# Stores given out some microseconds behind their producers in a graph-attention kernel of two layers

## The chip, the cores and the metric

The kernel runs on one core of one Trainium2 chip, in float32 throughout. Its time is the device time of one execution in microseconds (us). The core has five engines that run their own instruction streams in order: TensorE (PE, matrix products; its weight loads are listed apart as PEld), VectorE (DVE), ScalarE (ACT), GpSimd (POOL) and SyncE (SP), which computes nothing and here hands out nearly all DMA transfers. An instruction of one engine waits for another engine, or for a transfer, by a semaphore. PSUM is the small memory that PE writes its results to, SBUF the memory that all engines work in, DRAM the large memory outside.

## The reference

There are 128 batches of 128 nodes with 512 features. Layer 0 normalises, mixes the nodes by the adjacency matrix and multiplies by one weight. Layer 1 is masked attention with 8 heads and a projection, followed by a second normalisation.

```python
# layer 0
h = relu(layernorm(x))
x = x + (einsum('nm,bmd->bnd', adj, h) @ weight + bias)          # this x is called x1 below
# layer 1
h = relu(layernorm(x))                                           # called h1 below
q, k, v = split_heads(h @ w_qkv)                                 # 8 heads of 64
p = softmax(where(adj == 0, -inf, q @ k.T / 8))                  # the probabilities
o = (p @ v) @ w_proj + b_proj
x = x + o + layernorm(o) * gamma + beta
```

## The kernel before

The program is one long list of steps. `put(t, f, ...)` files a step under a nominal time `t` in us; at the end all steps are called in the order of these times, and each call appends its instructions to the engines' streams. So `t` sets only the order in every stream, SyncE's included, and not when anything runs. One batch has a slot of 17.8 nominal us; even and odd batches form pairs. Large products are done in a form with seven block products instead of eight, with sums of blocks made on POOL (`ysum`, `hsum`, `osum`).

A transfer appended to SyncE's stream in the step that also appends its producer stands there from that place on, and SyncE hands out nothing behind it until the producer is done. The parts that the change touches:

```python
    def exchange(t, b, dst=None):                 # 128x128 blocks are turned by a trip through DRAM
        w = b.shape[2]
        d = dram.tile([P, Q, w], F32, name=f"d{w}")
        nc.sync.dma_start(out=d, in_=b)           # L220: the store
        put(t, exchange_back, b if dst is None else dst, d)

    def exchange_back(dst, d):                    # L225: four reads, each for 32 partitions
        for q in range(Q):
            nc.sync.dma_start(out=dst[q * R:(q + 1) * R, :, :], in_=d[:, q, :].rearrange("(n r) w -> r n w", n=Q))

    def norm1_out(i, t, arg):                     # h1 of batch i
        h1 = H1[i] = work.tile([P, Q, C, R], F32, name="h1", bufs=4)
        nc.scalar.activation(h1..., X[i]..., AF.Relu, **arg)                        # L327
        exchange(t + 4.5, h1.rearrange("p q c r -> p q (c r)"))
        put(t + (1.5 if i >= AHEAD else 0), keep_x1, i)                             # AHEAD = 8

    def keep_x1(i):
        if i >= AHEAD:
            nc.gpsimd.tensor_tensor(X[i], X[i], beta_b, op=ALU.add)                 # L335
        X1D[i] = dram.tile([P, D], F32, name="x1d", bufs=20)
        nc.sync.dma_start(out=X1D[i], in_=X.pop(i))                                 # L337

    def softmax_mask(i, ps):                      # ps: scores in PSUM
        s = late(0) if spare(i) else work.tile([P, Q, H * R], F32, name="s", bufs=2)
        ...
        nc.vector.tensor_tensor(s..., ps[e]..., m4, op=ALU.add)                     # L401, then maximum L406

    def spare(i):
        return i > LATE + 2 and i % 2             # LATE = 120: batches 123, 125, 127

    def late(n):                                  # two places in a tile that is no longer in use
        if not LATER:
            t = work.tile([P, C, G, P], F32, name="h1T")...
            LATER.extend(t[:, n]... for n in range(2))
        return LATER[n]

    def softmax_divide(i, t, e, sm):
        nc.vector.reciprocal(sm, sm)                                                # L433
        nc.gpsimd.tensor_tensor(e, e, sm..., op=ALU.mult)                           # L435
        S[i] = late(1) if spare(i) else work.tile([P, Q, H * R], F32, name="sx", bufs=1)
        exchange(max(t + 5, read_at(i)), e.rearrange("p q h r -> p q (h r)"), S[i])

    def flip_probs(i):
        PT[i] = work.tile([P, 2 * C, P], F32, name="pT", bufs=2)
        nc.vector.transpose(PT[i]..., S.pop(i)...)                                  # L441

    def finish_out(i, t, arg):
        n = O.pop(i)
        nc.scalar.activation(n, n, AF.Identity, **arg)                              # L490
        put(t + 1.5, lambda: nc.gpsimd.tensor_tensor(n, n, gamma_b, op=ALU.mult))   # L491
        put(t + 3, finish_last, i, n, X1B.pop(i))

    def finish_last(i, n, x1):
        if i < AHEAD:
            nc.gpsimd.tensor_tensor(n, n, beta_b, op=ALU.add)                       # L496
        nc.gpsimd.tensor_tensor(n, n, x1, op=ALU.add)                               # L497
        nc.sync.dma_start(out=out[i], in_=n)                                        # L498
```

Other lines that the profile names: L285-286 the mixing (`pmix`), L300 the block products of layer 0 and of the projection (`pd`, `pz`), L263 and L306 DVE's emptying of their PSUM banks, L372 the block products for q, k and v (`pc`, `pz`), L376 ACT's emptying of them, L392 the scores (`ps`), L425 the exponentials, L450 the attention product (`po`), L468 whole products at the head and the tail, L159 the fetching of a weight block (`wq`), L479 the reloading of x1 (`x1b<-x1d`), L485 its sum with `o`.

Of the kernel before, what the change touches and what calls it, by code (L numbers as in the profile page):

```python
# [9 lines left out]
F32 = mybir.dt.float32  # L10
# [4 lines left out]
P = 128  # L15
# [5 lines left out]
def kernel(  # L21
# [30 lines left out]
    nc = tc.nc  # L52
    B, N, D = x.shape
    H = 8
    HD = D // H
    C = D // P
    G = 4
    Q, R = 4, 32
# [5 lines left out]
    work = ctx.enter_context(tc.tile_pool(name="work", bufs=2))  # L64
# [6 lines left out]
    LATER = []  # L71
    X, H0, YT, X1D, H1, H1T, WQ, QKT, V, S, PT, OT, O, X1B, LEFT0, LEFT1, LEFT2 = ({} for _ in range(17))
# [139 lines left out]

        return shifts, [dict(bias=shift[:, n:n + 1], scale=rs[:, n:n + 1]) for n in range(w)]

    def exchange(t, b, dst=None):


        w = b.shape[2]
        d = dram.tile([P, Q, w], F32, name=f"d{w}")
        nc.sync.dma_start(out=d, in_=b)  # L220
        put(t, exchange_back, b if dst is None else dst, d)

    def exchange_back(dst, d):
        for q in range(Q):
# [93 lines left out]
    def norm1(j, t):  # L318
        pair = 2 * j, 2 * j + 1
        shifts, args = stats_of([X[i] for i in pair])  # L320
        put(t + 3, shifts)
        for n, (i, arg) in enumerate(zip(pair, args)):
            put(t + 3 + n, norm1_out, i, t + 3 + n, arg)

    def norm1_out(i, t, arg):
        h1 = H1[i] = work.tile([P, Q, C, R], F32, name="h1", bufs=4)
        nc.scalar.activation(h1.rearrange("p q c r -> p c q r"), X[i].rearrange("p (c q r) -> p c q r", c=C, q=Q),  # L327
                             AF.Relu, **arg)
        exchange(t + 4.5, h1.rearrange("p q c r -> p q (c r)"))
        put(t + (1.5 if i >= AHEAD else 0), keep_x1, i)  # L330

    def keep_x1(i):

        if i >= AHEAD:
            nc.gpsimd.tensor_tensor(X[i], X[i], beta_b, op=ALU.add)  # L335
        X1D[i] = dram.tile([P, D], F32, name="x1d", bufs=20)
        nc.sync.dma_start(out=X1D[i], in_=X.pop(i))  # L337


    def flip(i):  # L340
# [43 lines left out]
    def scores(i, t):  # L384

        g, j = divmod(i, G)
        qk = QKT[g][j // 2]
        ps = [psum.tile([P, C, P], F32, tag="at", name=f"ps{e}", bufs=4) for e in range(2)]
        for c in range(C):
            for e in range(2):  # L390
                r = slice(e * HD, (e + 1) * HD)
                nc.tensor.matmul(ps[e][:, c, :], lhsT=qk[r, c, j % 2, :], rhs=qk[r, C + c, j % 2, :],  # L392
                                 start=True, stop=True)
        put(t + 1, softmax_mask, i, ps)

    def softmax_mask(i, ps):
        s = late(0) if spare(i) else work.tile([P, Q, H * R], F32, name="s", bufs=2)
        s = s.rearrange("p q (h r) -> p h q r", h=H)
        m4 = maskb.rearrange("p (q r) -> p q r", q=Q).unsqueeze(1).to_broadcast([P, C, Q, R])
        for e in range(2):  # L400
            nc.vector.tensor_tensor(s[:, e * C:(e + 1) * C], ps[e].rearrange("p c (q r) -> p c q r", q=Q), m4, op=ALU.add)  # L401
        put(softmax_at(i), softmax_max, i, softmax_at(i), s)
# [6 lines left out]
    def spare(i):  # L409
        return i > LATE + 2 and i % 2  # L410

    def late(n):

        if not LATER:
            t = work.tile([P, C, G, P], F32, name="h1T").rearrange("p (n c) j m -> p n (c j m)", n=2)
            LATER.extend(t[:, n].rearrange("p (q w) -> p q w", q=Q) for n in range(2))
        return LATER[n]

    def softmax_exp(i, t, s, shift):
        nc.scalar.mul(shift, shift, -scale)  # L420
        sm = stat.tile([P, H], F32, name="sm")

        def exps(heads):
            for h in heads:
                nc.scalar.activation(s[:, h], s[:, h], AF.Exp, bias=shift[:, h:h + 1], scale=scale,  # L425
                                     accum_out=sm[:, h:h + 1])

        exps(range(H // 2))
        put(t + 2, exps, range(H // 2, H))
        put(t + 4.2, softmax_divide, i, t + 4.2, s, sm)  # L430

    def softmax_divide(i, t, e, sm):
        nc.vector.reciprocal(sm, sm)  # L433
        e = e.rearrange("p h q r -> p q h r")
        nc.gpsimd.tensor_tensor(e, e, sm.unsqueeze(1).unsqueeze(3).to_broadcast([P, Q, H, R]), op=ALU.mult)  # L435
        S[i] = late(1) if spare(i) else work.tile([P, Q, H * R], F32, name="sx", bufs=1)
        exchange(max(t + 5, read_at(i)), e.rearrange("p q h r -> p q (h r)"), S[i])

    def flip_probs(i):
        PT[i] = work.tile([P, 2 * C, P], F32, name="pT", bufs=2)  # L440
# [40 lines left out]
    def finish(batches, t):  # L481
        shifts, args = stats_of([O[i] for i in batches])
        put(t + 3, shifts)
        for n, (i, arg) in enumerate(zip(batches, args)):
            put(t + 1 + 3 * n, lambda i=i: nc.gpsimd.tensor_tensor(X1B[i], X1B[i], O[i], op=ALU.add))  # L485
            put(t + 3 + 3 * n, finish_out, i, t + 3 + 3 * n, arg)

    def finish_out(i, t, arg):
        n = O.pop(i)
        nc.scalar.activation(n, n, AF.Identity, **arg)  # L490
        put(t + 1.5, lambda: nc.gpsimd.tensor_tensor(n, n, gamma_b, op=ALU.mult))  # L491
        put(t + 3, finish_last, i, n, X1B.pop(i))

    def finish_last(i, n, x1):
        if i < AHEAD:
            nc.gpsimd.tensor_tensor(n, n, beta_b, op=ALU.add)  # L496
        nc.gpsimd.tensor_tensor(n, n, x1, op=ALU.add)  # L497
        nc.sync.dma_start(out=out[i], in_=n)  # L498

# [6 lines left out]
    BEGIN, LAST, AHEAD = -3, B - G, 8  # L508
# [3 lines left out]
    def put(t, f, *a):  # L512
        count[0] += 1
        heapq.heappush(later, (t, count[0], f, a))

    def when(i, us):
        return i * SLOT + us if i >= 0 else i * SHORT + us * SHORT / SLOT

    def mix_at(i):
        return START + i * STEP if i < AHEAD else when(i - 10, (11.6, 9.2)[i % 2])  # L520
# [24 lines left out]
    LATE = LAST - G  # L545
    AT = {key: [] for key in "asQpD"}
    t, last = when(LATE, 0), ""
# [11 lines left out]
    def softmax_at(i):  # L559
        if i < LATE:  # L560
            return when(i, 0.5) if i % 2 else scores_at(i) + 3
        return TAIL + (5, 13, 26, 35, 58, 63.5, 70.5, 76)[i - LATE]

    def read_at(i):
        if i < LATE:
            return when(i + 1, 9) if i % 2 else 0
        return TAIL + (16, 24, 37, 46, 69, 74.5, 81.5, 87)[i - LATE]
# [6 lines left out]
    def attend_at(i):  # L574
        return when(i - i % 2 + 4, i % 2) if i < LATE - 4 else AT["a"][i - LATE + 4]
# [11 lines left out]
    for j in range(B // 2):  # L587
        a, b = 2 * j, 2 * j + 1
        i = a - 8
        if a < AHEAD:  # L590
            t = mix_at(a) - (8.5 if a else 5)
            put(t, norm0, j, t)
            for n in (a, b):
                t = mix_at(n) + 5.2
# [3 lines left out]
        else:  # L598
            t = when(i - 3, 5.2)
            put(t, norm0, j, t)  # L600
            t = when(i - 1, 12)
            put(t, pair_left, j, t, 2.5, YT, LEFT0, "ysum")
            run(lambda j=j: layer0(j), [when(i, p) for p in PAIR[0]])
            t = when(i, PAIR[0][6]) + 1.5
# [5 lines left out]
        i = a + 5  # L610
        t = attend_at(b) + 2
        if b < LAST:
            put(t, pair_left, j, t, 3.4 if i < LATE else 1.5, OT, LEFT2, "osum")
            n = 7 * (a - LATE + 4) // 2
# [3 lines left out]
        else:  # L618
            ends = []
            for n in (a, b):  # L620
                t = AT["D"][n - LAST]
# [8 lines left out]
    for g in range(B // G):  # L630
        i = g * G - 3
        t, gap = (START + 36.2, 1.4) if g == 0 else (when(i - 1, 13), 4) if i < LATE else (TAIL + 9.8, 2.2)
        put(t, group_left, g, t, gap)
        times = sorted(when(i + n, p) for n in range(G) for p in GROUP[(i + n) % 2] + ((13.1,) if n == 0 else ()))
        if i + G > LATE:
            n = sum(t < TAIL for t in times)
# [24 lines left out]
    while later:  # L661
        t, _, f, a = heapq.heappop(later)
# [30 lines left out]
```

## Time and profile before

| what | value |
|---|---|
| time, median of 3 runs | 2372.13 us (2368.23 to 2372.77) |
| span of the profiled execution | 2374.6 us |
| mean granted clock of TensorE | 0.996 |
| DMA moved | 518.86 MB, 218 GB/s |
| share of the time of 16 DMA engines taken by SyncE's queue | 68.7% |
| PE idle, by windows of 50 us: 0 to 150 us | 9.1 us |
| PE idle, 2250 us to the end | 23.3 us |

The profile's page lists busy time by engine, the waits of each engine with what ended them, the chain of work that ended last, and groups of instructions by source line. A line of the waits reads "engine tile line <- releaser tile line: us in total, times, longest us". SPq is the queue of SyncE. An entry such as "[4.89 <-DMA d<-h1T]" gives the idle time of the engine just before that instruction and what ended it. "a<-b" names the tile written and the tile read.

### The profile page before, as it was taken

To read this page: it belongs to the slowest core of one execution; us is meant where nothing else is said; L and a number is where in the kernel's file an instruction comes from. 1 tells how busy PE (TensorE), PEld (TensorE's weight loads), DVE (VectorE), ACT (ScalarE), POOL (GpSimd) and SP (SyncE) were. 2 spreads that over 40 slices of the span, in tenths; PEclk is the share of its full clock that TensorE was granted. 3 is DMA by queue.
4 is the path that set the end of the run, shared out by engine and by line. 5 is a ranking of instruction groups with operands and counts; after the bars stand their busy time and mean duration, and the time that the engine had idled before them with its cause. 6 is when DMAs were issued, how large, how long until landed. Compare 5 with 4: busy or idle time off the path is not lost.

```text
span 2374.6 us, 43019 instructions
## 1 busy us (share of the span) xinstructions
PE 2332.3 (98%) x14131; PEld 2052.9 (86%) x14131; DVE 1462.2 (62%) x3287; ACT 1066.1 (45%) x3202; POOL 1671.4 (70%) x1592
## 2 busy tenths in 40 slices
PE   8999999999999999999999999999999999999996
PEld 7888888888888888888888888888888888888885
DVE  6556656665665566666666665666666666566654
ACT  3444444454444444444544444444445444444442
POOL 4467777777677766776776777677777767866667
PEclk9999999999999999999999999999999999999998
DMA  7576676766766767677677767677676676676664
GB/s 261 186 221 204 220 231 214 232 222 211 227 218 215 225 211 231 217 220 235 214 216 233 218 217 229 215 227 222 218 232 216 217 233 213 222 229 208 213 209 139
DMA packets 395885, 518.86 MB, mean 218 GB/s; under 512 B 39696, under 2 KB 247696, under 8 KB 395664
## 3 DMA queue, kind: packets, MB, share of 16 engines
q1 hardware_dynamic: 394976, 515.53, 68.7%
q8 instruction: 113, 1.85, 0.3%
q14 instruction: 108, 0.88, 0.1%
q10 hardware_dynamic: 688, 0.59, 0.1%
HBM read 345.05 MB, written 170.92 MB: 217 GB/s over the span
## 4 chain that ended last, share of the span: by engine, by line
PE 83%; DMA 4%; POOL 4%; DVE 4%; ACT 2%; SPq 2%; issue 1%; POOLq 0%; DVEq 0%
PE pc L372 36%; PE pd L300 24%; PE pz L372 6%; PE ps L392 4%; PE pmix L286 4%; PE po L450 4%; PE pz L300 4%; DMA sx<-d 2%; SPq L225 2%; DMA x1b<-x1d 1%; ACT s L425 1%; PE pd L468 1%; POOL x1b L485 1%; DVE pT L441 1%; DVE st L201 1%
## 5 line engine op out<-in xcount | busy, mean ns | idle before, releaser
L206 POOL TENSOR_TENSOR rs<-ve,minus_half 128x2 f32<-128x2 f32 (+1 forms) x194 | 135.6, 699 | 618.0 <-DVE ve L204 617.3
L372 PE MATMUL pc<-hsum,wq 128*128 128x256 f32 x1984 | 468.3, 379 | 3.4 <-POOL o L491 1.8
L372 PEld LDWEIGHTS pc<-hsum,wq 128*128 128x128 f32 x1984 | 376.6, 190 | 55.4 <-POOL o L491 2.2
L425 ACT ACTIVATE s<-s,mx 128x128 f32<-128x128 f32 x1000 | 387.8, 389 | 4.2
L435 POOL TENSOR_TENSOR s<-s,sm 128x1024 f32<-128x1024 f32 x125 | 239.1, 1913 | 38.4 <-DVE sm L433 38.2
L300 PE MATMUL pd<-wp_sb,osum 128*128 128x256 f32 x992 | 254.2, 379 | 1.4 <-DVE sm L433 1.4
L300 PE MATMUL pd<-w_sb,ysum 128*128 128x256 f32 x960 | 246.3, 379 | 0.0
L663 ACT COPY oT<-po 128x512 f32<-128x512 f32 x128 | 74.9, 586 | 372.0 <-PE po L450 372.0
L372 PE MATMUL pc<-wq,hsum 128*128 128x256 f32 x992 | 238.1, 383 | 1.0 <-ACT s L425 1.0
L372 PE MATMUL pc<-h1T,wq 128*128 128x256 f32 x992 | 237.6, 382 | 0.0
L441 DVE STREAM_TRANSPOSE pT<-sx 128x1024 f32<-128x1024 f32 x125 | 155.0, 1240 | 125.0 <-DMA sx<-d 123.0
L372 PEld LDWEIGHTS pc<-wq,hsum 128*128 128x128 f32 x992 | 186.6, 190 | 29.3 <-ACT s L425 1.3
L372 PEld LDWEIGHTS pc<-h1T,wq 128*128 128x128 f32 x992 | 185.9, 190 | 27.9 <-DMA wq<-in_L_gnn_w_qkv_dram 0.3
L306 DVE TENSOR_TENSOR o<-pd,bp_b 128x256 f32<-128x256 f32 x248 | 103.0, 416 | 171.7 <-PE pd L300 171.4
L300 PEld LDWEIGHTS pd<-wp_sb,osum 128*128 128x128 f32 x992 | 184.0, 190 | 24.5 <-issue 1.8
L376 ACT COPY qkT<-pc 128x512 f32<-128x512 f32 x256 | 144.5, 575 | 128.6 <-PE pc L372 128.4
L300 PEld LDWEIGHTS pd<-w_sb,ysum 128*128 128x128 f32 x960 | 177.9, 190 | 21.7
L490 ACT ACTIVATE o<-o,shift,rs 128x512 f32<-128x512 f32 x128 | 103.4, 808 | 196.4 <-POOL osum L234 123.0
L401 DVE TENSOR_TENSOR s<-ps,maskb 128x512 f32<-128x512 f32 x250 | 155.4, 683 | 56.4 <-PE ps L392 55.6
L425 ACT ACTIVATION_READ_ACCUMULATOR s<-s,mx 128x1 f32 x1000 | 187.2, 187 | 0.0
L201 DVE BATCH_NORM_STATS2 st<-x 128x6 f32<-128x512 f32 x256 | 171.9, 672 | 4.4 <-DMA x<-in_x_dram 4.4
L485 POOL TENSOR_TENSOR x1b<-x1b,o 128x512 f32<-128x512 f32 x120 | 152.9, 1275 | 25.7 <-DMA x1b<-x1d 25.2
(141 smaller groups left out, 4691.8 us busy)
## 6 DMA issues: line engine op xcount, KB each, us to landing
wq<-wt SPq DMA_DIRECT2D x372, 256.0 KB, 4.0
wq<-in_L_gnn_w_qkv_dram SPq DMA_DIRECT2D x279, 256.0 KB, 3.7
d<-s SPq DMA_DIRECT2D x125, 512.0 KB, 3.0
sx<-d SPq DMA_DIRECT2D x500, 128.0 KB, 3.0
x<-in_x_dram SPq DMA_DIRECT2D x128, 256.0 KB, 4.5
d<-h SPq DMA_DIRECT2D x128, 256.0 KB, 2.9
x1d<-x SPq DMA_DIRECT2D x128, 256.0 KB, 3.1
h<-d SPq DMA_DIRECT2D x512, 64.0 KB, 2.3
```

Of the source, the lines that this page charges most:

```text
L201: nc.vector.bn_stats(st, src)
L206: nc.gpsimd.tensor_tensor(rs, ve, minus_half[:, :w], op=ALU.pow)
L300: nc.tensor.matmul(p[:, 0, :], lhsT=left[k][:, c, :], rhs=w_sb[:, k, c, :], start=first and c == 0, stop=last and c == 1, skip_group_check ...
L306: nc.vector.tensor_tensor(results[n], p[:, 0, :], addend[n // 2][:, n % 2 * F:(n % 2 + 1) * F], op=ALU.add)
L372: nc.tensor.matmul(p[:, half, :], lhsT=lhsT, rhs=rhs, start=first and half == 0 and c == 0, stop=last and c == 1, skip_group_check=True)
L376: nc.scalar.copy(results[n], p)
L401: nc.vector.tensor_tensor(s[:, e * C:(e + 1) * C], ps[e].rearrange("p c (q r) -> p c q r", q=Q), m4, op=ALU.add)
L425: nc.scalar.activation(s[:, h], s[:, h], AF.Exp, bias=shift[:, h:h + 1], scale=scale, accum_out=sm[:, h:h + 1])
L435: nc.gpsimd.tensor_tensor(e, e, sm.unsqueeze(1).unsqueeze(3).to_broadcast([P, Q, H, R]), op=ALU.mult)
L441: nc.vector.transpose(PT[i].rearrange("p h (q r) -> p q h r", q=Q), S.pop(i).rearrange("p q (h r) -> p q h r", h=H))
L485: put(t + 1 + 3 * n, lambda i=i: nc.gpsimd.tensor_tensor(X1B[i], X1B[i], O[i], op=ALU.add))
L490: nc.scalar.activation(n, n, AF.Identity, **arg)
```

## The change

The change files the stores as steps of their own, so that they stand in SyncE's stream some nominal us behind the step that appends their producer: the h1 store 1.2, the store of the probabilities 2.2, the x1 store 2 (0 for the first 8 batches), the result's store 5 (1.5 for the last 8 batches). The reads stay at the times they had. It is for SyncE to hand out, in the meantime, transfers that are ready. Apart from that, the probabilities of the odd batches at the end (123, 125, 127) get more places: a tile `yT`, no longer used by then, gives two more, so that 125 and 127 have their scores in places of their own, and the reloaded copies take the two old ones in turn.

```diff
-    def exchange(t, b, dst=None):
+    def exchange(t, t_back, b, dst=None):
         w = b.shape[2]
         d = dram.tile([P, Q, w], F32, name=f"d{w}")
-        nc.sync.dma_start(out=d, in_=b)
-        put(t, exchange_back, b if dst is None else dst, d)
+        put(t, nc.sync.dma_start, d, b)
+        put(t_back, exchange_back, b if dst is None else dst, d)
@@ norm1_out
-        exchange(t + 4.5, h1.rearrange("p q c r -> p q (c r)"))
-        put(t + (1.5 if i >= AHEAD else 0), keep_x1, i)
-
-    def keep_x1(i):
+        exchange(t + 1.2, t + 4.5, h1.rearrange("p q c r -> p q (c r)"))
+        t += 1.5 if i >= AHEAD else 0
+        put(t, keep_x1, i, t)
+
+    def keep_x1(i, t):
         if i >= AHEAD:
             nc.gpsimd.tensor_tensor(X[i], X[i], beta_b, op=ALU.add)
         X1D[i] = dram.tile([P, D], F32, name="x1d", bufs=20)
-        nc.sync.dma_start(out=X1D[i], in_=X.pop(i))
+        put(t + (2 if i >= AHEAD else 0), nc.sync.dma_start, X1D[i], X.pop(i))
@@ softmax_mask
-        s = late(0) if spare(i) else work.tile([P, Q, H * R], F32, name="s", bufs=2)
+        s = late((i - LATE - 1) // 2 * (i > LATE + 3)) if spare(i) else work.tile([P, Q, H * R], F32, name="s", bufs=2)
@@ late
         if not LATER:
             ...
+        if n > 1 and len(LATER) == 2:
+            LATER.extend(work.tile([P, C, 2, P], F32, name="yT").rearrange("p c j m -> p c (j m)") for _ in range(2))
         return LATER[n]
@@ softmax_divide
-        S[i] = late(1) if spare(i) else work.tile([P, Q, H * R], F32, name="sx", bufs=1)
-        exchange(max(t + 5, read_at(i)), e.rearrange("p q h r -> p q (h r)"), S[i])
+        S[i] = late((i - LATE - 1) // 2 % 2) if spare(i) else work.tile([P, Q, H * R], F32, name="sx", bufs=1)
+        exchange(t + 2.2, max(t + 5, read_at(i)), e.rearrange("p q h r -> p q (h r)"), S[i])
@@ finish_out, finish_last
-        put(t + 3, finish_last, i, n, X1B.pop(i))
-
-    def finish_last(i, n, x1):
+        put(t + 3, finish_last, i, t + 3, n, X1B.pop(i))
+
+    def finish_last(i, t, n, x1):
         ...
         nc.gpsimd.tensor_tensor(n, n, x1, op=ALU.add)
-        nc.sync.dma_start(out=out[i], in_=n)
+        put(t + (5 if i < LATE else 1.5), nc.sync.dma_start, out[i], n)
```

Line numbers below are those of the kernel before; in the changed kernel they stand a few lines lower, and every delayed store has the line of the loop that calls the steps (L667).

## The prediction

> **What bounds the kernel now.** First the page's busy times: is there an engine with nothing left to give?
>
> ```profile
> PE 2332.3 (98%) x14131; PEld 2052.9 (86%) x14131; DVE 1462.2 (62%) x3287; ACT 1066.1 (45%) x3202; POOL 1671.4 (70%) x1592
> ```
>
> TensorE (PE) is busy for 2332.3 of 2374.6 us, so all its idle time together is 42.3 us. The change alters no matmul, so it can win only from those 42.3 us. A 2% gain would be 47.4 us, more than all of them.
>
> Second, who PE waited for, by the list of PE's waits (total, times, longest):
>
> ```profile
> PE pd L300 <- DVE x L263: 9.9, 11, 1.9
> PE po L450 <- DVE pT L441: 3.5, 1, 3.5
> PE pd L300 <- DVE o L263: 3.4, 1, 3.4
> PE pc L372 <- POOL hsum L234: 3.1, 2, 1.6
> PE pc L372 <- ACT qkT L376: 2.9, 1, 2.9
> PE pc L372 <- POOL o L491: 1.8, 1, 1.8
> ```
>
> One wait comes back 11 times, always at the first matmul of a layer-0 product that needs a PSUM bank which VectorE (DVE) has yet to empty. The others are single events at the head or the tail. Between about 180 us and 2210 us the recurring wait is PE's only one.
>
> Third, the chain that ended last, around one of the 11 (start, duration, what), from 284 to 306 us:
>
> ```profile
> 284.68 4.64 DMA x1b<-x1d
> ...
> 295.82 1.28 POOL o L497
> 297.10 0.02 issue
> 297.12 0.34 SPq L498
> ...
> 299.22 3.25 DMA sx<-d
> ...
> 302.55 1.25 DVE pT L441
> 303.80 0.58 DVE v L263
> 304.38 0.34 DVE x L263
> 304.72 0.04 issue
> 304.76 1.13 PE pd L300 x4
> ```
>
> Read it backwards. PE waits for DVE's add, which stands in DVE's program behind the transpose of the probabilities, which waits for their reload (sx<-d). That reload is not late because of its data: SyncE issued its store at 277.14. It stands in SyncE's queue behind the store of a result (L498), which cannot go before GpSimd (POOL) has finished that result at 297.1. SyncE had issued its last transfer before it at 290.00 (timeline), so it stood for 6.7 us at a store that nobody was waiting for. SyncE's own waits say the same in total:
>
> ```profile
> SPq L498 <- POOL o L497: 304.8, 123, 8.2
> SPq L220 <- POOL s L435: 225.9, 123, 21.7
> SPq L220 <- ACT h L327: 137.7, 62, 10.5
> ```
>
> [...] So a store with an unfinished producer holds up everything behind it, and the profiled window starts when the wait is over. The trace agrees: L498 shows 0.34 us, and the 6.7 us stand ahead of it. [...] a transpose waiting 4.33 us for sx delays the add behind it. [...]
>
> **The change part by part: the steady part.** The changed program has the same instructions in the same order on PE, DVE, ScalarE (ACT) and POOL, but for the name of a tile. Only SyncE's order moves. In each pair of batches the sequence "out, read sx, weight, out, store s" becomes "read sx, weight, out, store s, weight, out". In the group above the read is then held up only by its single sx buffer, free when the preceding transpose (291.28, 1.24 us) ends at 292.5. Four issues take about 1.8 us, the last leaves near 294.0, and 3.25 us later (same chain) the data lands at 297.3. DVE would come to that transpose at 298.2 (its preceding add starts at 297.81 and takes 0.42). PE stalled for 1.81 us, so the transpose may start as late as 302.55 - 1.81 = 300.7 without a stall. The margin is 2.5 us on a transfer of 3.0 median and 6.0 at worst (the answer for sx). So I expect all 11 stalls to go.
>
> Their worth I take from PE's rhythm, not from the 9.9 us, for a restart costs something too: the first group after a stall shows 1.13 us, others 1.03, and the next group starts 0.97 instead of 0.86 later. PE's score products (ps, L392) start once in a pair, and the undisturbed intervals alternate between 35.22 and 36.95 us (2066.36, 2101.58, 2138.53). Every interval of the first kind from 250 us on is 35.22. I sum what the second kind has above 36.95, from 212.76 to 2211.58: 1.06 + 2.07 + 0.30 + 2.14 + 0.06 + 0.87 + 1.07 + 1.93 + 0.51 + 0.65 + 1.10 + 0.56 + 0.12 + 0.88 = 13.3 us. The large ones are the 11 waits; 0.30, 0.06 and 0.12 are smaller traces of the same. Gain: 13.3 us.
>
> **The h1 and x1 stores.** With h1 behind its producer by 1.2 and x1 by 2 us, the new order is "h1 store, weight, h1 store, s store, x1 store, read, x1 store, read". Around 275 us the last read is issued near 282 instead of 284. No PE wait hangs on it: 0. At the head (batches 0 to 7) x1 is now stored ahead of h1, which moves an h1 store from 31.3 to about 34 us; its read stood at 36.95 behind other things anyway. I count 0, with 0.5 us either way.
>
> **The tail.** Three kinds of places matter; batch numbers count from 0 to 127.
>
> ```profile
> 2321.83 1.29 DVE L401 TENSOR_TENSOR h1T<-ps,maskb 128x512 f32<-128x512 f32 x2 [4.89 <-DMA d<-h1T]
> 2324.63 2.07 PE L300 MATMUL pd<-wp_sb,oT 128*128 128x256 f32 x4 [3.40 <-DVE o L263]
> 2347.36 1.25 DVE L441 STREAM_TRANSPOSE pT<-h1T 128x1024 f32<-128x1024 f32 x1 [4.90 <-DMA h1T<-d]
> 2348.66 1.97 PE L450 MATMUL po<-pT,v 128*64 128x128 f32 x16 [3.51 <-DVE pT L441]
> ```
>
> In the first line the scores of batch 127 go into the place in which batch 125's probabilities still wait to be stored. DVE stands for 4.89 us and PE behind it for 3.40. The change gives 127 a place of its own. DVE can then start near 2317.5, when the last scores are done (PE from 2315.95 for 1.64 us). PE's 3.40 us go, plus some 0.7 us that the slow group after it (2.58 us instead of 1.89) shows. But DVE soon meets the transpose of batch 124, whose read was issued from 2316.28 to 2318.03: with 3.0 to 3.5 us it lands at 2321.0 to 2321.5. The transpose (1.24) and the add (0.65) end at 2322.9 to 2323.4, while PE would come to that bank at 2321.07 + 0.86 = 2321.95. So 1.0 to 1.5 us come back: net about 3.
>
> The last probabilities set the end. After the transpose at 2347.36, POOL's stream of additions and multiplications runs nearly gapless to 2371.7. Their chain (DVE maximum, ACT exponentials, DVE reciprocal, POOL product, store, read) starts at 2323.04 with the maximum of batch 126, which could start at about 2318.8: 4.2 us earlier. Its last product can move by 4, for PE, DVE and ACT around it move by 3 to 4 as well. Then the store of batch 127: before, it went at 2337.28, as its product ended; now a result's store stands before it, held by POOL's L497, which ends 1.27 us after the product. Its read was held until 2342.14, 4.86 us after the store, by two result stores and two reloads. Now the store lands about 3 us after a start 1.3 us later, so the read goes some 4.4 after the product: even or slightly better. Gain at the end: 4.0 us. The 3.51 us wait on the last line stays; both its ends move.
>
> What I leave at 0: the 1.79 and 1.41 us stalls at 2275 and 2281 us. In the first PE's bank is emptied by an ACT copy (2274.92, 0.56) held behind a normalisation waiting for DVE; in the second the read waits for its single sx buffer, freed by a transpose at 2273.6. Neither is touched. The head's waits (POOL hsum, ACT qkT) stay.
>
> Sum: 13.3 + 4.0 = 17.3; 2372.1 - 17.3 = 2354.8, rounded to 2355 us.
>
> **The rivals.** *A new blocker takes the old one's place.* The result stores still stand in one queue; the later one now stands right ahead of the even batch's sx read, the weight fetch ahead of the second h1 store. For it: SyncE waits for PE at weight fetches for 213.0 us in all. Against it: results finish (297.1 and 301.6) before the s store that now follows (303.47), and the weight fetch is nominally 4 steps ahead. If half the stalls come back: 2362. *The transfers themselves are the limit:* the DMA engines are 69% busy, and in one of the 11 the first of four read issues took 1.03 us with nothing else before it. If earlier reads only meet the x1b and x loads in the same burst, a third of the 13.3 us stays: 2359. *The tail gains nothing,* as PE's work there is held by its own order: 2359. *More is gained:* the 3.51 us wait shrinks too, or the 1.79 and 1.41: down to 2349. *A slip at the head or in the tail's order* could cost 3 to 5 us, which the steady part would still outweigh.
>
> **Range and chances.** The centre takes nearly all of 13.3 and 4.0; both rivals of half a gain give 2362 to 2364; everything going well gives 2349. Range 2349 to 2364. For faster by over 2% the time must fall under 2324.7, below PE's own 2332.3 busy us: 0.01. Slower by over 2% needs 47 us of new stalls: 0.01. Within 2%: 0.98.
>
> **What would show it.** Right: no recurring PE wait on DVE x L263, intervals of 35.22 and 36.95 nearly throughout, SyncE's wait at result stores far below 304.8 us, no 4.89 us wait at batch 127's scores, PE still about 2332 us busy. Wrong: that same PE wait at about 10 us with another SyncE releaser, or a new PE wait on weights, or a last transpose no earlier relative to the start of the tail.

## The result and the profile after

The changed kernel takes 2355.28 us (median; 2353.87 to 2360.04), the kernel before 2371.1 beside it: ratio 0.9938, 95% interval 0.9921 to 0.9956. The profiled execution is the longest of those runs, 2358.1 us; the others span 2352.1 to 2353.5 at a slightly higher granted clock (the share of its full clock that TensorE was given: 0.997 and 0.998, here 0.996). The profiled execution of the kernel before took 2376.43 us, 4.3 above the median of the other three, so what the two profiles differ by, stretch by stretch, is not exactly what the medians differ by: these give 15.8 us. A second measurement of the same kernel (below, e11) gave 2355.91 us, ratio 0.9926 [0.9913, 0.9938], 17.8 us under the kernel before beside it.

First the page of the kernel after: the busy times, and further down the shares of the chain that ended last.

```profile
PE 2327.8 (99%) x14131; PEld 2053.4 (87%) x14131; DVE 1473.4 (62%) x3287; ACT 1065.8 (45%) x3202; POOL 1670.0 (71%) x1592
...
PE 93%; DMA 2%; POOL 1%; issue 1%; DVE 1%; SPq 1%; ACT 0%; POOLq 0%; DVEq 0%; ACTq 0%
```

PE does the same 14131 matmuls, and is idle for 30.3 us of its span instead of 42.3. Of the last chain 93% is now PE (83% before): where the chain used to hop from PE to DVE, a transfer, SyncE and POOL and back, it now stays on PE.

Second, PE's waits of the kernel after (engine, tile and line, releaser: total, times, longest).

```profile
PE po L454 <- DVE pT L445: 4.2, 1, 4.2
...
PE pc L373 <- POOL x1b L489: 1.8, 1, 1.8
PE pd L300 <- DVE sm L437: 1.4, 1, 1.4
```

The recurring wait (DVE x L263, 9.9 us in 11 pieces) and the 3.4 us on DVE o L263 are gone. What is left are single events at the head and in the tail; the largest, before the last attention product, has grown from 3.5 to 4.2.

Third, SyncE's own waits of the kernel after.

```profile
SPq L667 <- POOL s L439: 300.4, 98, 18.3
SPq L159 <- PE pc L373: 273.1, 99, 6.2
...
SPq L667 <- POOL o L501: 33.6, 14, 7.7
```

SyncE does not wait less. It waited 304.8 us at result stores and now 33.6; but it waits 300.4 (225.9) at stores of probabilities and 273.1 (213.0) at weight fetches. It now stands where nothing urgent is behind it.

The steady part, around the group that the prediction worked out (the pair whose score products start at 284.43 us in this trace): SyncE's timeline of the kernel after (start, duration, what).

```profile
290.99 2.02 SPq L225 DMA_DIRECT2D sx<-d  x4
...
295.35 0.36 SPq L667 DMA_DIRECT2D out_dram<-o  x1
301.70 0.32 SPq L667 DMA_DIRECT2D d<-s  x1
```

And DVE's timeline of the same stretch.

```profile
289.73 1.23 DVE L445 STREAM_TRANSPOSE pT<-sx 128x1024 f32<-128x1024 f32 x1
...
296.59 1.23 DVE L445 STREAM_TRANSPOSE pT<-sx 128x1024 f32<-128x1024 f32 x1
...
298.84 0.43 DVE L263 TENSOR_TENSOR x<-pd,x 128x256 f32<-128x256 f32 x1 [0.17 <-PE pd L300]
```

The read of sx leaves 0.03 us after the transpose that frees its place (289.73 + 1.23 = 290.96), ahead of the result's store. The second transpose starts without a wait (no bracket behind it), and the add on the last line waits for PE, not PE for it. Four reads took 2.6 to 3.4 us from issue to landing.

Where the time came from, by the starts of the score products (first, then the last of the steady rhythm, then the end of the span):

| stretch | before | after | gained |
|---|---|---|---|
| start to first score products | 78.93 | 79.77 | -0.84 |
| first to 2211.58 / 2198.41 | 2132.65 | 2118.64 | 14.0 |
| from there to the end | 163.0 | 159.7 | 3.3 |
| sum | 2374.6 | 2358.1 | 16.5 |

The same stretches in the profile of e11: 78.28, 2117.72 and 157.7, so gains of 0.65, 14.9 and 5.3.

### The profile page after: what moved, and what is told of

Its sections match the earlier page's. It is cut to its first block, busy times and chain, and to the rows that moved or that the text cites. A ratio compares the mean times of both kernels' runs of the same rounds, so it can differ in the third digit from the quotient of the medians.

```text
span 2358.1 us, 43096 instructions
## 1 busy us (share of the span) xinstructions
PE 2327.8 (99%) x14131; PEld 2053.4 (87%) x14131; DVE 1473.4 (62%) x3287; ACT 1065.8 (45%) x3202; POOL 1670.0 (71%) x1592
## 4 chain that ended last, share of the span: by engine, by line
PE 93%; DMA 2%; POOL 1%; issue 1%; DVE 1%; SPq 1%; ACT 0%; POOLq 0%; DVEq 0%; ACTq 0%
PE pc L373 41%; PE pd L300 26%; PE pz L373 7%; PE ps L393 5%; PE po L454 5%; PE pmix L286 4%; PE pz L300 4%; DMA d<-s 0%; SPq L225 0%; POOL rs L206 0%; POOL x L489 0%; DMA d<-h 0%; DMA x<-in_x_dram 0%; DMA sx<-d 0%; DMA oT<-in_L_gnn_w_qkv_dram 0%
## 5 line engine op out<-in xcount | busy, mean ns | idle before, releaser
L667 ACT COPY oT<-po 128x512 f32<-128x512 f32 x128 | 74.8, 585 | 371.9 <-PE po L454 371.9
L377 ACT COPY v<-pc 128x512 f32<-128x512 f32 x128 | 74.3, 581 | 214.6 <-PE pc L373 214.6
L277 POOL TENSOR_TENSOR x<-x,b_b 128x512 f32<-128x512 f32 x128 | 161.7, 1264 | 2.4 <-ACT h L274 2.4
```

The lines of the kernel that those rows point to most:

```text
L277: nc.gpsimd.tensor_tensor(x_, x_, b0_b, op=ALU.add)
L377: nc.scalar.copy(results[n], p)
```

## The experiments

Every ratio is against the kernel before. "Stalls" are, as in the prediction, the sum of what PE's intervals between score products have above 36.95 us (and above 35.22 for the other kind) from about 210 us on; the kernel before has 13.5 by this count, the kernel after 0.6, all of it in one place. "Tail" is from the start of the last but one group of score products (2314.46 before, 2301.37 after) to the end of the span: 60.1 before, 56.7 after.

**e1: the result stores alone.**

```diff
-        nc.sync.dma_start(out=out[i], in_=n)
+        put(t + (5 if i < LATE else 1.5), nc.sync.dma_start, out[i], n)
```

> The kernel before with the result stores alone put behind (5 and 1.5 us); h1, x1 and probability stores and the last places as before. My theory, that one store held up the sx read: all recurring PE waits on DVE x L263 go, PE's intervals fall to 35.22 and 36.95, the tail keeps its 3.4 us wait: 13.3 us faster, ratio about 0.994. Rival, that the gain is shared with the other stores (SyncE waited 225.9 us at probability stores and 137.7 us at h1 stores): about half of the stalls stay, 5 to 7 us faster. Rival, that the transfers themselves were slow: about 9 us faster.

2363.33 us, ratio 0.9959 [0.9946, 0.9971]. Stalls 0.8; no wait on DVE x. Tail 60.8, and the wait that the missing place causes is there in PE's waits:

```profile
PE pd L300 <- DVE o L263: 4.2, 1, 4.2
```

So the result stores alone take the steady stalls away. The time shows less than the 13.3 us expected: 9.7 us by the ratio, and its interval leaves the expected 0.994 just out. A likely reason, not shown, is that the 13.3 us were counted in one long execution of the kernel before; e4 below, which doesn't differ from it in time, has 10.1 by the same count.

**e2: the places for the last probabilities alone.**

```diff
-        s = late(0) if spare(i) else ...
+        s = late((i - LATE - 1) // 2 * (i > LATE + 3)) if spare(i) else ...
```

(with the two further places and their turn, as in the change; all stores at their producers)

> The kernel before with the places for the last probabilities alone; all stores as before. My theory: the steady part with its 11 waits is unchanged, the wait of 4.89 us at the scores of batch 127 goes, the tail from the last scores of the steady part to the end shrinks by 3 to 4.5 us: ratio about 0.998 to 0.9985. Rival, that the tail is held by PE's own order or by the last read: within 1 us of before.

2369.56 us, ratio 0.9983 [0.9975, 0.9991]. Stalls 14.2, tail 57.0, the wait on DVE o gone. The places alone carry the tail. 0.9959 x 0.9983 = 0.9942, close to the whole change (0.9938 and 0.9926).

**e3: the change without the delay of the result stores.**

```diff
-        put(t + (5 if i < LATE else 1.5), nc.sync.dma_start, out[i], n)
+        nc.sync.dma_start(out=out[i], in_=n)
```

> The changed kernel with its result stores put back to where their producers stand; h1, x1 and probability stores behind and the places stay. My theory: the recurring waits come back in full and the 13.3 us are lost, the tail's 3 to 4 us stay: 3 to 4 us faster than before, ratio about 0.9985. Rival, that h1, x1 and probability stores carry a part: 8 us faster or more.

2366.57 us, ratio 0.9971 [0.996, 0.9981]. Stalls 7.4, tail 57.2. PE waits for DVE x again (6 times, 5.3 us in all), and SyncE stands 289.0 us at result stores. How much of the steady gain is lost is less sure: by the stall count about half, by the medians of e2 and e3 all but 3.0 us of it, with intervals that overlap. Whether the other delays do something for the same stall is therefore open.

**e4: two places for sx instead of one, in the kernel before.**

```diff
-        ... else work.tile([P, Q, H * R], F32, name="sx", bufs=1)
+        ... else work.tile([P, Q, H * R], F32, name="sx", bufs=2)
```

> The kernel before with two places for the reloaded probabilities (sx) instead of one; the order of SyncE's queue as before. My theory: the read still stands behind the result's store, so the steady part does not change; only the wait of 1.41 us in the tail, whose read waited for the single place, may go: 0 to 2 us faster. Rival, that the single sx place binds the read: the 13.3 us of the steady part come, ratio about 0.994.

2372.54 us, ratio 0.9997 [0.9988, 1.0005]. Stalls 10.1, tail 60.5. PE still waits 12 times on DVE x (6.5 us in all). The second buffer did not help the read, which still stood behind another transfer in its queue: it left 8.69 us after the score products (8.99 before).

**e5: the h1 and x1 stores alone.**

```diff
-        exchange(t + 4.5, h1)                      # store here
+        exchange(t + 4.5, h1, lag=t + 1.2)         # store 1.2 behind
-        nc.sync.dma_start(out=X1D[i], in_=X.pop(i))
+        put(t + (2 if i >= AHEAD else 0), nc.sync.dma_start, X1D[i], X.pop(i))
```

> The kernel before with the h1 and x1 stores alone put behind (1.2 and 2 us). Theory: they do nothing for the sx read by themselves; but the h1 reads leave SyncE about 1.2 us earlier, so x1 is reloaded and the result finished earlier, and the result's store holds SyncE for less time. That should give the half that the runs without result stores behind showed: PE's intervals sum to about 7 us above 35.22 and 36.95 instead of 13.5, 4 to 6 us faster. Rival, that the half came from the probability stores put behind by 2.2 us: no change in the sum, within 1.5 us of before.

2420.86 us, ratio 1.0191 [1.017, 1.0213]: 46 us slower. Both expectations fell. From PE's waits of e5:

```profile
PE pd L303 <- DVE x L266: 41.6, 29, 3.6
```

It is the old stall, more often and longer. The order in SyncE's queue tells why. SyncE's timeline of e5 (score products at 440.17):

```profile
431.48 0.32 SPq L221 DMA_DIRECT2D d<-s  x1
431.89 0.38 SPq L667 DMA_DIRECT2D d<-h  x1
...
433.19 0.63 SPq L667 DMA_DIRECT2D d<-h  x1
...
435.14 1.81 SPq L228 DMA_DIRECT2D h<-d  x4
...
437.53 2.60 SPq L228 DMA_DIRECT2D h<-d  x4
...
440.65 0.43 SPq L483 DMA_DIRECT2D x1b<-x1d  x1
```

And of the kernel before (score products at 432.40):

```profile
426.10 4.89 SPq L225 DMA_DIRECT2D h<-d  x8
...
431.52 0.43 SPq L479 DMA_DIRECT2D x1b<-x1d  x1
```

The probability store d<-s has kept its place; the h1 stores, moved back a step, are now behind it. SyncE sends nothing from 426.15, the end of its last issue, to 431.48, for it waits for POOL's product (in all 385.4 us at this store, 225.9 before). Then come the h1 stores and an x1 store, to 434.38. The h1 reads and the x1b reload behind them come late: x1b 0.48 us after the score products instead of 0.88 before them. A delayed store had met a store that was not delayed. SyncE's waits at result stores grow too, from 304.8 us to 337.1.

**e6: result stores issued by GpSimd, in the kernel before.**

```diff
-        nc.sync.dma_start(out=out[i], in_=n)
+        nc.gpsimd.dma_start(out=out[i], in_=n)
```

> The kernel before with the result stores handed out by GpSimd, whose last addition makes the result, and not by SyncE; nothing is put behind. Theory, that what costs is SyncE standing still: the read of sx no longer has a store ahead of it, the recurring stalls go as they do with the stores behind, less what handing out costs GpSimd in each of 128 batches: 8 to 13 us faster. Rival, that GpSimd (70% busy, and the one that makes the sums and the probabilities) loses about 1 us a batch and passes it on: as slow as before or slower, with new PE waits on hsum or osum.

2378.06 us, ratio 1.0016 [1.001, 1.0023]: slower, although the steady stalls fall to 3.2 and the last scores come 5.2 us earlier (2309.27). One issue in POOL's timeline of e6:

```profile
299.32 0.61 POOL L498 DMA_DIRECT2D out_dram<-o  x1 [0.30 <-POOL o L497]
```

This issue holds POOL for 0.61 us and waits 0.30 for POOL's own result (the rival's 1 us a batch was the author's estimate); over all 128 POOL's busy time goes from 1671.4 to 1753.6 us, 82.2 / 128 = 0.64 each. The tail, which hangs on POOL's stream, takes 65.6 us instead of 60.1: from the start of the last attention product to the end of the span it is 32.2 us instead of 26.0. Ahead of the tail, at 2270 us, PE has a new wait of 4.85 us for a copy of ACT, which had itself stood 7.55 us for POOL's sum `x1b` (L485). The issue time was only moved, from SyncE (0.34 us for such a store before) to an engine that needs it, but with the store its wait left SyncE's queue, and most of the stall with it (13.5 us to 3.2), which is more than issue time.

**e7: the change, with the last eight result stores 5 us behind as well instead of 1.5.**

```diff
-        put(t + (5 if i < LATE else 1.5), nc.sync.dma_start, out[i], n)
+        put(t + 5, nc.sync.dma_start, out[i], n)
```

> The changed kernel with the result stores of the last 8 batches 5 us behind too, instead of 1.5: the store and the read of batch 127's probabilities then stand ahead of two result stores. Theory: that store goes as its product ends, 1.6 us earlier than at 2321.38, its landing of about 3 us ends the wait, PE's wait of 4.24 us before the last attention product becomes about 2.6, and the end comes 1 to 1.7 us earlier. Rival, that GpSimd's stream of additions sets the end: less than 0.5 us.

2353.56 us, ratio 0.9913 [0.9899, 0.9926]; span 2351.0, stalls none, tail 53.8. It is the fastest kernel here by its median, 1.7 us under the changed one; the intervals of the two still overlap. Its tail is read further below.

**e8: the change, with the first eight h1 stores at their producers.**

```diff
+        if t is None: nc.sync.dma_start(out=d, in_=b)          # batches 0 to 7
```

> The changed kernel with the h1 stores of the first 8 batches back at their producers, ahead of the x1 stores, as before. Theory: the head loses 0.8 us by the change because an h1 store of the first group moved behind a wait for weight sums; PE's wait on hsum at 47 us goes from 2.39 back to about 1.5, the first scores start near 78.9 instead of 79.8: 0 to 1 us faster. Rival, that the head only varies from run to run: wait and start spread as much among runs of one order, no change.

2356.36 us, ratio 0.9925 [0.9911, 0.9938], not to be told from the change. In the profile the head is as expected: PE's wait on POOL hsum near 47 us is 1.41 instead of 2.39, and the second group's h1 read leaves at 36.63 instead of 38.11. First scores came at 78.57 us; but the changed kernel itself gave 79.77 in one execution and 78.28 in the other, so a microsecond there is within what the head varies by itself.

**e9: the probability stores alone, with the places, which their delay needs.**

```diff
-        exchange(max(t + 5, read_at(i)), e, S[i])
+        exchange(max(t + 5, read_at(i)), e, S[i], lag=t + 2.2)
```

> The kernel before with the probability stores alone put behind by 2.2 us, and the places for the last ones, which that needs. SyncE's order becomes h1 store, h1 store, x1 store, weight, x1 store, probability store, eight h1 reads, so the h1 reads and the x1 reload leave when they did before. Theory, that the half of the stalls which went without the result stores behind came from the x1 reload leaving 1.2 us earlier, and that this needs the x1 stores behind and the probability store behind the h1 stores, both: the steady part stays (sum about 13 us), only the places count, 3 to 4 us faster. Rival, that the probability store's place alone gave the half: sum about 7 us, 6 to 8 us faster.

2432.0 us, ratio 1.0266 [1.0241, 1.0291]: 58 us slower, and again both expectations fell. PE's and SyncE's waits of e9:

```profile
PE pd L303 <- DVE x L266: 46.4, 36, 3.9
```

```profile
SPq L340 <- POOL x L338: 170.3, 110, 3.9
```

Here the probability store has slid behind both x1 stores, right ahead of all eight h1 reads, which before followed the x1 store directly. SyncE now waits 170.3 us at x1 stores (53.2 before), and 360.0 at result stores (304.8). Behind the second of them stand the probability store's issue (0.42 us in one such place) and reads that then take 5.48 us to issue (4.89 before), which fits the x1b reload leaving 0.8 us later in the table below. The revised theory after e5 and e9 is this: it isn't a store's delay that counts but what it puts in front of what. With the result's store ahead of the sx read, that read's time hangs on the whole queue upstream: h1 reads, then x1b reload, then POOL's sum with it, the finished result, its store, the read.

**e10: everything together: the change with e7's tail, e8's head and two sx places.**

> The changed kernel with three more edits: result stores of the last 8 batches 5 us behind, h1 stores of the first 8 batches at their producers as before, and two sx places. Expected from the single runs: 1.7 us from the tail's order, 0.3 to 1.4 us from the second sx place (the wait near 2268 us), 0 to 0.8 us at the head: 2 to 4 us faster than the changed kernel, about 2352. Rival, that the rest is the granted clock and not waits: no better than the tail's order alone, 2353.5.

2353.99 us, ratio 0.9919 [0.9906, 0.9933]; stalls none, tail 55.3. That is no better than e7, as the rival had it, and 1.9 us under e11, which was measured beside it and has the same tail.

**e11: the changed kernel once more.**

> The changed kernel as it is, beside the two above on the same chip, as their measure: ratio near 0.9938, about 2355 to 2358 us. If its profile has no longer the wait on a weight sum near 312 us and PE's wait near 2268 us varies, these are chance of single executions and not the change's.

2355.91 us, ratio 0.9926 [0.9913, 0.9938], span 2353.7, stalls none, tail 55.3. The small wait at 312 us in the first profile (0.46) isn't there, and the wait near 2268 us is 0.51 instead of 1.36. So both are chance of single executions, and so are 1.4 us of the tail.

**e12: e9 with the result stores behind as well.** The test of the revised theory: the harmful edit is left in, and only the store that couples the read to the queue upstream is moved.

```diff
  (e9)
-        nc.sync.dma_start(out=out[i], in_=n)
+        put(t + (5 if i < LATE else 1.5), nc.sync.dma_start, out[i], n)
```

> The kernel before with the stores of the probabilities and of the results behind their producers, and the places for the last probabilities; the h1 and x1 stores stay at their producers. Without the result stores this same edit was 58 us slower than before. Theory (only the place of the read of the odd batch's probabilities decides, and with the result store behind it that place is fixed by its buffer): the read goes out 6.55 us after the start of the pair's score products and its transpose starts at 12.16, the PE waits on DVE x (46.4 us in the run without the result stores) go, although the x1 reload still leaves up to 1 us after that start; 13 + 3 to 4 us faster than before: ratio 0.993 to 0.995. Rival (the delayed probability store costs by the later h1 reads, whatever the result store does): PE's waits on DVE x stay above 10 us and the time stays above that of the kernel before, ratio over 1.00.

2363.38 us, ratio 0.9954 [0.9938, 0.997]; stalls 0.2, tail 56.9. One edit takes 68.6 us off e9. PE's waits of e12, then SyncE's:

```profile
PE po L455 <- DVE pT L446: 4.7, 1, 4.7
PE pc L375 <- POOL hsum L237: 3.4, 2, 1.8
```

```profile
SPq L340 <- POOL x L338: 171.6, 112, 3.9
```

SyncE still stands 171.6 us at x1 stores, as in e9, and PE doesn't feel it. The ratio is just above the expected 0.993 to 0.995: this run has two weight waits at the head (1.44 and 1.33 us at 116 and 150 us) that the changed kernel lacks. Why they come is open.

The rows below are offsets in us from the start of a pair's score products, as median and largest, for the pairs between 350 and 2200 us (of the pair's two x1b reloads, the first). They show the coupling and how it is cut:

| kernel | x1b reload issued | sx read issued | its transpose | DVE waits for it (median) | time, us |
|---|---|---|---|---|---|
| e9, probabilities only | -1.07 / 0.99 | 9.98 / 11.46 | 15.64 / 16.98 | 3.40 | 2432.0 |
| e5, h1 and x1 only | -1.27 / 0.96 | 9.44 / 11.62 | 15.07 / 18.09 | 2.83 | 2420.86 |
| before | -1.90 / -0.36 | 8.99 / 10.55 | 13.98 / 16.63 | 1.74 | 2371.1 |
| e4, before with two sx places | -1.91 / -0.42 | 8.69 / 9.90 | 13.65 / 15.88 | 1.41 | 2372.54 |
| e3, all but results | -3.01 / -1.02 | 8.70 / 9.54 | 13.95 / 15.48 | 1.71 | 2366.57 |
| e12, e9 and results | -1.19 / 0.23 | 6.56 / 6.68 | 12.16 / 12.58 | 0 | 2363.38 |
| e1, results only | -1.91 / -0.56 | 6.56 / 6.56 | 12.16 / 12.16 | 0 | 2363.33 |
| after | -3.11 / -1.16 | 6.55 / 6.56 | 12.16 / 12.28 | 0 | 2355.28 |

In the first five rows a later x1b goes, roughly, with a later read, most clearly by the largest values. In the last three the read goes at 6.55 whatever x1b does, because the place for sx and no longer the queue fixes it. In e5 and e9 x1b leaves 0.6 and 0.8 us later than before. That e3 has fewer stalls because its x1b leaves 1.1 us earlier would fit, but isn't shown: e4, whose x1b leaves as before, has the same median of the read as e3.

## Why the prediction was right, point by point

**The steady part (13.3 us predicted).** Right in mechanism; the size is right for the execution that it was counted in. By the prediction's own count 12.9 us went (13.5 less 0.6), and all 13.5 in e11; from the first score products to 2211.58 it was 14.0, as a 0.98 us wait at 148 us is gone too. The prediction had the read at 292.5 and DVE's transpose at 298.2, that is 6.5 and 12.2 us after the score products at 285.99; the trace has 6.55 and 12.16. That these waits go in e1 and are back in e3 makes the result store the cause, and e12 shows that it is this store's place ahead of the read and not the load of SyncE that counts. But the prediction took what it counted in an execution of 2376.43 us from a median of 2372.1, and e1 gained 9.7 us where the count promised 13.3. That the sum still came out (17.3 us, against 15.8 and 17.8 by the two measurements) is in part luck: what made up for the difference isn't resolved.

**The h1 and x1 stores (0 predicted).** Right for the change as a whole: e1 and e2 together (0.9942) leave 1 to 4 us for these and the probability stores by the ratios, less than the intervals resolve. What the prediction missed is that this 0 holds only together. "No PE wait hangs on it" was true beside the other delayed stores. In the kernel before, the same edit costs 46 us (e5). Moved one without the other, the h1 or the probability store lands in front of the other's readers. Moved together, without the result stores, they cost nothing (e3), and with the result stores moved the probability store alone costs PE nothing either (e12). The h1 and x1 stores were not tried with the result stores alone.

**The head (0 with 0.5 either way).** The first scores came 0.84 us later in one execution and 0.65 earlier in the other, and e8 made no difference in time. Not resolved beyond that.

**The tail (4.0 us predicted; 3.3 in the profile above, 5.3 in e11's, 3.2 by the medians of e2).** The place was the cause (e2), and the sum is as good as the scatter allows, but the terms of the sum were mis-sized. PE's timeline of the kernel after, from the last attention product:

```profile
2331.04 1.98 PE L454 MATMUL po<-pT,v 128*64 128x128 f32 x16 [4.24 <-DVE pT L445]
...
2336.52 2.49 PE L472 MATMUL pd<-wp_sb,oT 128*128 128x256 f32 x10
```

And the granted clock of this stretch (the stretch, its length, busy time with counts of PE, PEld, DVE, ACT and POOL, clock, DMA share, GB/s):

```profile
2331.00:2336.50 5.50, 5.46 (x24) 4.44 (x25) 1.80 (x5) 1.27 (x2) 3.73 (x4) 0.50 0.19 58
```

From 2319.34 to 2344.06, around the 3.40 us wait, PE needed 24.72 us before and for the same groups 19.46 after: 5.26 less, not "PE's 3.40 us go, plus some 0.7 us". The idle piece with its edges was 3.56, and both groups behind it ran slow (1.87 instead of 0.86 to the next start, 2.42 instead of 1.73: 1.01 + 0.69). The "1.0 to 1.5 us" that were to "come back" at batch 124's transpose didn't: PE has no wait there between its last scores at 2302.86 and the line at 2331.04.

"The 3.51 us wait on the last line stays; both its ends move" is the step that was off. The ends moved by different amounts: PE comes 5.26 us earlier, the transpose 4.53, so the wait became 4.24. What held the probabilities' side was the store of batch 127: its product ends at 2319.72, but the store goes at 2321.38, behind a result store that waits for POOL. From product to read it took 4.85 us, where the prediction had 4.4.

Then the half clock behind the wait lasted longer. By the clock records of the traces it was 0.50 for 3.41 us before and for 6.83 us after, and from that product to the group of ten (the second line) it took 4.32 us before and 5.48 after. So 4.53 - 1.16 = 3.4 of the 5.26 arrive. The wait's length does not decide this alone: in e11 the same kernel waited 4.07 us there, the half clock lasted 3.41 us, the group of ten started 4.49 us after the product, and the tail was 1.4 us shorter. e7 removes the result store from in front of batch 127's. SyncE's and PE's timelines of e7, and its clock:

```profile
2315.96 0.34 SPq L667 DMA_DIRECT2D d<-yT  x1
```

```profile
2325.00 1.09 PE L454 MATMUL po<-pT,v 128*64 128x128 f32 x16 [2.27 <-DVE pT L445]
```

```profile
2325.00:2328.00 3.00, 3.00 (x25) 2.62 (x26) 1.77 (x5) 0.59 (x1) 1.26 (x2) 1.00 0.18 67
```

The store leaves 0.03 us after its product ends at 2315.93, the read at 2319.04, 3.1 us after it instead of 4.85; the wait is 2.27, the clock stays at 1.00, and the group of ten starts 2.86 us after the product. From the last scores to the last product e7 needs 26.34 us (after 28.18), then 2.86 (5.48), then 23.14 to the end (21.58): some 1.6 us are given back, since POOL's additions and multiplications, now nearly gapless (from 2326.74 us on one wait of 0.42 us, where the kernel after has 0.95 and 0.49), become what the end waits for. So of the 2.9 us between the tails of e7 and of the profile above, some 1.5 (53.8 against e11's 55.3) come from the order, and the rest is what two executions of the changed kernel differ by. e10 shows the same from the other side: its wait of 2.73 us was followed by 5.49 us to the group of ten at clock 0.50, so with the same order of the last stores its tail is 1.5 us longer than e7's.

**The rivals.** *A new blocker takes the old one's place:* not in the change (SyncE waits 300.4 us at probability stores, PE loses nothing by it), but fully real in e5 and e9, which are 46 and 58 us slower. *The transfers themselves are the limit:* no; the reads landed in 2.6 to 3.4 us and stalls of 0.8 are left in e1. *The tail gains nothing:* no (e2). *More is gained:* the wait of 3.51 grew in the change and was shortened (to 2.27) by e7's order. The 1.79 us wait at 2275 us stayed (1.78 after). The 1.41 us stall that the prediction put on the single sx place was indeed that: it is gone with two places (e4, e10), and it was still there in the change (1.36, and 0.51 in e11).

## What to carry to other kernels

A queue that issues transfers in program order is a schedule of its own (here SyncE stood for 304.8 us at result stores, with the sx reads behind them): look for the transfer with the longest waits that nobody needs soon, and put it behind those that are ready and needed, before thinking of more buffers (ratio 0.9997 in e4) or of another engine's queue (1.0016 in e6). A move is worth only what it puts in front of what, so parts of a reordering that is free as a whole can be harmful alone; measure the parts, and count a coupling as cut only when the release time no longer varies with what is upstream. Before valuing a wait of PE that lasts some 2 us or more, look at the granted clock of the matmuls behind it (here 1.00 after 2.27 us in e7, 0.50 after 2.73 us in e10).

## What the runs showed of the hardware

What followed a PE wait here went with its length, but not with that alone. Of the waits of 0.3 us and more in the 14 profiles (from 60 us on), none of the 144 under 1.95 us was followed by a halved clock, 6 of the 16 from 1.95 to 2.65 us were, and 21 of the 22 longer ones (2.73 to 4.85 us; the exception is one of 3.42 in e6). By the clock records the half clock lasted 3.41 us in 17 of these 27 cases (behind the waits of 3.40 and 3.51 us before, for instance) and 6.83 us in 10 (behind that of 4.24 after), and it began anywhere from 2.3 us before the end of the wait to 1.1 us after it. So the group directly behind shows it only in part: four matmuls that take 1.03 us usually took 2.07 in the kernel before after a wait of 3.40, and 1.13 in e9 after one of 1.96, where the clock fell 1.05 us after the wait.

In e5 PE's waits on DVE x grew by 31.7 us and its busy time by 11.1 (2343.4 against 2332.3); the two make 42.8 of the 44.3 us by which the span grew. The mean granted clock was 0.993 (0.996 before).

In e6 a DMA issue by GpSimd held that engine for 0.61 us, against 0.34 in SyncE's row for such a store in the kernel before.
